# Layer 0's closing stage: the last pair's out_proj and transposes earlier, in_proj in two places, 24 unread products on TensorE

## The chip, the cores and the metric

One core of a Trainium2 chip runs the whole program. The time is device microseconds (us) of one execution, given as the median of several. The profile is of one further execution. TensorE (PE) does matrix products and transposes and writes PSUM. VectorE (DVE), ScalarE (ACT) and GpSimd (POOL) do elementwise work and reductions; SyncE (SP) issues most of the transfers. Each engine takes its own instructions in order.

## The reference, cut to what matters

Two layers run over an image of 64 x 64 tokens of 96 channels. Each layer is a mixer with a residual, and then a small quantized MLP with a residual:

```
x = x + L0_conv(ln_c(x))          # layer 0: in_proj 96 -> 192 + 192, depthwise 3x3 conv, SiLU,
                                  # four selective scans, layernorm, * silu(z), out_proj 192 -> 96
t = x + L0_ffn(ln_t(x))           # 96 -> 384, relu, 384 -> 96; operands rounded to 8 bits
x = t + L1_conv(ln_c(t))          # layer 1: in_proj, full 3x3 conv 192 -> 192, SiLU, four scans,
x = x + L1_ffn(ln_t(x))           #          * silu(z), out_proj; then the MLP again
```

The change lies at the end of layer 0: the layernorm of its mixer, the gate, out_proj, its MLP, and then the layernorm and the in_proj of layer 1.

## The kernel before

The 4096 tokens are 8 chunks of 512. `self.res` keeps the residual of all of them in SBUF, tokens on partitions. `back0` closes layer 0. It works on pairs of chunks: pair 0 is chunks 0 and 2, pair 1 is 1 and 3, pair 2 is 4 and 6, pair 3 is 5 and 7. A loop over `s` from -1 to 4 staggers the pairs: in step `s`, the mixer's statistics of pair `s + 1` stand beside out_proj and MLP of pair `s`, and beside layer 1's transposes and in_proj of pair `s - 1`.

What a step calls, with the lines of before:

- `centred(s + 1)`: products with a matrix of 1/192 (tiles `m`, L1075 and L1077) give the mean, DVE subtracts it, ACT squares (`sq`), POOL multiplies by the gate.
- `gated_sums(s)`: the product with the out_proj weights (tiles `oc`, L1110 and L1112), copied to SBUF by ACT (`ot`).
- `gated_out(c)`: four transposes (`o`, L1124), four DVE instructions that scale and add to the residual (L1127), and then `norm_chunk` for the MLP (tiles `lnmb`, `lnxcb`, `lnsqb`, `lnvb`, `lnrb`, `lnxnb`) with a cast on POOL (`xb`, L1981).
- `to_layer1(c)`: four transposes of a chunk that has its MLP behind it (`tr`, L188), a copy by ACT (`xt`, L189) and a store that SP issues (L1135).
- `keep_in_proj(c)`: layer 1's in_proj (`in`, L331), two products of 96 x 512 for a chunk; ACT copies one and DVE the other into the padded image `pad` (L333).
- `variance(s + 1)`: three products that sum the squares (`ov`, L1093), a root on ACT (`osd`), two small transfers, a reciprocal on DVE (`or`).
- `mlp_turn`, `mlp_up`, `mlp_down`: four transposes (`tf`), three products of 96 x 512 bf16 (`h`, L2000) with casts and relu on ACT, DVE and POOL, and twelve small fp8 products (`of`, L2020). After `mlp_down` the residual is added on DVE, and `norm_chunk` makes layer 1's input (tiles `lnmc` to `lnxnc`).

TensorE's order is the order of the source (`keep` enters each product into it). DVE, ACT, POOL and SP are ordered by the compiler's scheduler, so moving a call moves instructions on these engines too. PSUM tiles rotate in small pools: three buffers for `m` and `in` (tag `a`), two for `oc` and `h` (tag `h`), two for `ov`, `o` and `of` (tag `o`), one for `tr` and `tf` (tag `t`). A tile waits until the last reader of the one before it in its buffer is done.

After the loop, layer 1 begins with the product `spread4p` (L1197) and its convolution (`cw`, L1230), which reads the padded image of all chunks.

Of the kernel before, what the change touches and what calls it, by code (L numbers as in the profile page):

```python
# [28 lines left out]
F32 = mybir.dt.float32  # L29
# [10 lines left out]
P = 128  # L40
# [8 lines left out]
CH = 512  # L49
# [71 lines left out]
class Net:  # L121
# [897 lines left out]
    def back0(self):  # L1019

        tc = self.tc
        self.xn_d = self.scratch("xn1", [CD, L])
        with ExitStack() as ctx:
            self.tp = ctx.enter_context(tc.tile_pool(name="af0", bufs=3))
            self.lp = ctx.enter_context(tc.tile_pool(name="al0", bufs=2))  # L1030
            self.pa = ctx.enter_context(tc.tile_pool(name="ps_a0", bufs=3, space=PSUM))
            self.po = ctx.enter_context(tc.tile_pool(name="ps_o0", bufs=2, space=PSUM))
            self.ph = ctx.enter_context(tc.tile_pool(name="ps_h0", bufs=2, space=PSUM))
            self.pt = ctx.enter_context(tc.tile_pool(name="ps_t0", bufs=1, space=PSUM))
            self.w_in = self.w_in1
            n = NCH // 2
            self.sq, self.factor, self.xb, self.xn, self.xt, self.hid = {}, {}, {}, {}, {}, {}

            def chunks(s):
                c0 = s // 2 * 4 + s % 2  # L1040
                return (c0, c0 + 2) if 0 <= s < n else ()

            for s in range(-1, n + 1):
                if s + 1 < n:
                    self.centred(s + 1, chunks(s + 1))
                if 0 <= s < n:
                    self.gated_sums(s, chunks(s))
                for k in range(2):
                    for c in chunks(s - 1)[k : k + 1]:
                        self.to_layer1(c)  # L1050
                    for c in chunks(s)[k : k + 1]:
                        self.gated_out(c)
                for c in chunks(s - 1):
                    self.keep_in_proj(c)
                sums = self.variance(s + 1, chunks(s + 1)) if s + 1 < n else iter(())
                next(sums, None)
                for c in chunks(s):
                    self.mlp_turn(0, c)
                    self.mlp_up(0, c, lambda: next(sums, None))
                for _ in sums:  # L1060
                    pass
                for c in chunks(s):
                    self.mlp_down(0, c)
                    self.xn[c] = self.norm_chunk(self.lp, c, self.eps6, F32, f"c{c}")

    def keep(self, instruction):
        self.tc.keep_in_program_order(instruction)
# [1042 lines left out]
```

## Time and profile before

| | |
|---|---|
| median of 8 runs | 1451.32 us |
| lowest and highest | 1445.39 and 1462.72 us |
| the profiled execution | 1454.14 us, span 1452.3 us, mean TensorE clock 0.852 |
| `back0` in that execution | about 123.8 to 247.2 us from the start of the span |

The span runs from the first to the last instruction. In `back0` a step of the loop takes 24 to 27 us, and the last, which has only pair 3's layer 1 work left, 13.4 us (233.8 to 247.2). PEclk is the TensorE clock that was granted, 1.00 being full speed; in this stage the records show only 1.00 and 0.50, so a value between them is the share of time at either. A count of products in the trace is in passes: an f32 product appears as two MATMUL records. Idle time in square brackets is that of the engine just before an instruction, with what ended it.

### The profile page before, as it was taken

The numbers are of one execution on the slowest core, as the hardware profiler recorded it, in microseconds if no ns is written. First come the engines' busy times: TensorE is split into PE (matmuls) and PEld (weight loads), VectorE is DVE, ScalarE is ACT, GpSimd is POOL, SyncE is SP. The second block draws the span as 40 slices with busy tenths as digits, with TensorE's granted clock in tenths as the row PEclk, the third lists the DMA queues.
The fourth block names the chain that finished last, engine by engine and source line by source line (L and its number), as shares of the span: only waits on it lengthen the run. The fifth ranks groups of instructions, "written<-read, shape, count | busy, mean of one in ns | idle before, by whom it ended". The sixth has DMA issues, their size and how long they took to land. (4 is left out here: it accounts for less than half of the span.)

```text
span 1452.3 us, 12894 instructions
## 1 busy us (share of the span) xinstructions
PE 1156.0 (80%) x3976; PEld 467.2 (32%) x3976; DVE 1155.0 (80%) x887; ACT 909.9 (63%) x1099; POOL 785.4 (54%) x461
## 2 busy tenths in 40 slices
PE   7997777999991677787776777677778888899875
PEld 4532233333330222222222222222223333344343
DVE  6494674033169999999999999999999999999875
ACT  4455653044266677777777776777777777778444
POOL 1002321000005877687778776787878677885445
PEclk8999886999995889888888888878889998978855
DMA  2143000024059453735374457455555547442201
GB/s 64 47 143 72 11 17 17 15 54 124 22 164 286 140 185 127 221 111 181 127 246 124 137 175 226 136 161 178 170 182 157 169 135 239 147 129 89 71 2 42
DMA packets 68850, 183.19 MB, mean 126 GB/s; under 512 B 21488, under 2 KB 35460, under 8 KB 61956
## 3 DMA queue, kind: packets, MB, share of 16 engines
q1 hardware_dynamic: 67480, 182.00, 40.4%
q8 instruction: 33, 0.54, 0.2%
q10 hardware_dynamic: 1292, 0.28, 0.1%
q14 instruction: 45, 0.37, 0.1%
HBM read 155.98 MB, written 20.47 MB: 121 GB/s over the span
## 5 line engine op out<-in xcount | busy, mean ns | idle before, releaser
L1573 POOL TENSOR_TENSOR hss<-h1s,xws 128x1024 f32<-128x1024 f32 x96 | 224.5, 2375 | 135.5 <-PE hs L1581 135.5
L1557 ACT ACTIVATE da<-dt1s,a 128x1024 f32<-128x1024 f32 x168 | 187.9, 1119 | 139.9 <-DVE xws L1568 83.9
L1581 PE MATMUL hs<-hss,ident 128*128 128x512 f32 x376 | 216.3, 659 | 53.5 <-POOL hss L1573 33.1
L1568 DVE TENSOR_TENSOR_SCAN xws<-da,xws 128x1024 f32<-128x1024 f32 x96 | 224.2, 2335 | 10.4 <-DVE xws L1568 2.7
L1557 ACT ACTIVATE da<-dt0s,a 128x1024 f32<-128x1024 f32 x168 | 187.4, 1115 | 70.6 <-DVE xws L1568 52.3
L1581 PE MATMUL hs<-h0s,ident 128*128 128x512 f32 x376 | 203.5, 624 | 0.1
L1568 DVE TENSOR_TENSOR_SCAN h1s<-da,h1s,xws 128x1024 f32<-128x1024 f32 x72 | 169.2, 2350 | 11.0 <-ACT da L1557 2.3
L1581 PEld LDWEIGHTS hs<-hss,ident 128*128 128x128 f32 x376 | 70.5, 204 | 186.3 <-issue 81.8
L1396 POOL TENSOR_TENSOR dun<-u,dtn 128x512 f32<-128x512 f32 x4 | 5.9, 1482 | 197.2 <-DVE dtn L1293 107.6
L1581 PEld LDWEIGHTS hs<-h0s,ident 128*128 128x128 f32 x376 | 76.0, 203 | 100.3 <-issue 95.8
L1602 PE MATMUL acc<-hc2s,fold 128*32 128x512 f32 x128 | 47.5, 831 | 61.3 <-POOL hc2s L1591 58.2
L1602 PE MATMUL acc<-hc0s,fold 128*32 128x512 f32 x128 | 46.8, 820 | 52.9 <-POOL hc0s L1591 52.9
L1602 PE MATMUL acc<-hc1s,fold 128*32 128x512 f32 x128 | 45.5, 798 | 51.3 <-POOL hc1s L1591 51.3
L1541 POOL TENSOR_TENSOR x1s<-x1s,dus 128x1024 f32<-128x1024 f32 x32 | 75.0, 2360 | 9.1 <-DMA x1s<-bc 9.1
L1541 POOL TENSOR_TENSOR x2s<-x2s,dus 128x1024 f32<-128x1024 f32 x32 | 75.2, 2364 | 6.2 <-DMA x2s<-bc 6.2
L1568 DVE TENSOR_TENSOR_SCAN x0s<-da,x0s 128x1024 f32<-128x1024 f32 x32 | 74.7, 2335 | 4.3 <-ACT da L1557 1.9
L1568 DVE TENSOR_TENSOR_SCAN x1s<-da,x1s 128x1024 f32<-128x1024 f32 x32 | 74.7, 2335 | 3.6 <-ACT da L1557 1.0
L1568 DVE TENSOR_TENSOR_SCAN x2s<-da,x2s 128x1024 f32<-128x1024 f32 x32 | 74.7, 2335 | 3.3 <-ACT da L1557 0.7
L1581 PE MATMUL hs<-x0s,ident 128*128 128x512 f32 x128 | 67.4, 609 | 0.3 <-DVE x0s L1568 0.3
L1581 PE MATMUL hs<-x1s,ident 128*128 128x512 f32 x128 | 66.4, 601 | 0.0
L1541 POOL TENSOR_TENSOR x0s<-x0s,dus 128x1024 f32<-128x1024 f32 x28 | 65.8, 2363 | 0.0
L1253 PE MATMUL cv<-pad,cw 128*128 128x512 f32 x144 | 64.3, 598 | 0.0
(346 smaller groups left out, 2355.0 us busy)
## 6 DMA issues: line engine op xcount, KB each, us to landing
c0s<-bc SPq DMA_DIRECT2D x184, 128.0 KB, 2.5
c1s<-bc SPq DMA_DIRECT2D x184, 128.0 KB, 2.6
x2s<-bc SPq DMA_DIRECT2D x32, 512.0 KB, 4.9
x0s<-bc SPq DMA_DIRECT2D x28, 512.0 KB, 3.9
x1s<-bc SPq DMA_DIRECT2D x28, 512.0 KB, 6.6
dus<-du SPq DMA_DIRECT2D x20, 512.0 KB, 7.0
dt1s<-dt SPq DMA_DIRECT2D x40, 256.0 KB, 6.4
dt0s<-dt SPq DMA_DIRECT2D x40, 256.0 KB, 4.8
```

What stands on the lines that cost most here:

```text
L1253: keep(nc.tensor.matmul(t, cw[0][:, tap, 0:P], v, start=tap == 0, stop=False))
L1396: keep(nc.gpsimd.tensor_tensor(dun, u[1][:, m], dtn, ALU.mult))
L1541: keep(nc.gpsimd.tensor_tensor(x, x, du[:, part[j]], ALU.mult))
L1557: keep(nc.scalar.activation(das[i, s], dts[o][:, part[j]], AF.Exp, scale=self.a6[:, g, k : k + 1]))
L1568: keep(nc.vector.tensor_tensor_scan(to, da, x, start, ALU.mult, ALU.add))
L1573: keep(nc.gpsimd.tensor_tensor(cols(hs)[:, w, :], grid(h1)[:, w, :], grid(xw)[:, w, :], ALU.add))
L1581: keep(nc.tensor.matmul(t, self.ident, x[:, chunk(m)], start=x is hs, stop=x is xs[i % 3]))
L1602: keep(nc.tensor.matmul(to, self.fold4, src, start=k == 0, stop=k == NK - 1))
```

## The change

Steps -1, 0, 2, 3 and 4 are edited; step 1 is as before.

- In step 2, `gated_sums` of pair 3 is called between the two `mlp_down` calls, and no longer at the start of step 3.
- In step 3, `gated_out` of both chunks of pair 3 stands ahead of `to_layer1` of pair 2 (before, they alternated, `to_layer1` first). The in_proj of chunk 4 follows its transposes at once; the in_proj of chunk 6 stands after the MLP's first part of chunk 5.
- In step 4, the in_proj of a chunk follows its own transposes at once (before, both chunks were transposed first).
- `awake(n)` issues `n` products of 128 x 128 f32 into a PSUM tile of tag `a` that nothing reads: 4 in step -1 after `centred`, 6 in step 0 after the first product of `variance`, 4 in step 3 after `gated_out`, and 10 in step 4 ahead of the transposes.

```diff
             for s in range(-1, n + 1):
+                last = s == n - 1
                 if s + 1 < n:
                     self.centred(s + 1, chunks(s + 1))
-                if 0 <= s < n:
+                if 0 <= s < n and not last:
                     self.gated_sums(s, chunks(s))
-                for k in range(2):
-                    for c in chunks(s - 1)[k : k + 1]:
+                if s == -1:
+                    self.awake(4)
+                if last:
+                    for c in chunks(s):
+                        self.gated_out(c)
+                    self.awake(4)
+                    for c in chunks(s - 1):
                         self.to_layer1(c)
-                    for c in chunks(s)[k : k + 1]:
-                        self.gated_out(c)
-                for c in chunks(s - 1):
-                    self.keep_in_proj(c)
+                        if c == chunks(s - 1)[0]:
+                            self.keep_in_proj(c)
+                elif s == n:
+                    self.awake(10)
+                    for c in chunks(s - 1):
+                        self.to_layer1(c)
+                        self.keep_in_proj(c)
+                else:
...
                 sums = self.variance(s + 1, chunks(s + 1)) if s + 1 < n else iter(())
                 next(sums, None)
+                if s == 0:
+                    self.awake(6)
                 for c in chunks(s):
                     self.mlp_turn(0, c)
                     self.mlp_up(0, c, lambda: next(sums, None))
+                    if last and c == chunks(s)[0]:
+                        self.keep_in_proj(chunks(s - 1)[1])
...
                 for c in chunks(s):
+                    if s == n - 2 and c == chunks(s)[1]:
+                        self.gated_sums(n - 1, chunks(n - 1))
                     self.mlp_down(0, c)
...
+    def awake(self, products):
+
+        t = self.pa.tile([P, CH], F32, tag="a", name="awake")
+        for _ in range(products):
+            self.keep(self.nc.tensor.matmul(t[:, 0:P], self.mean, self.ident, start=True, stop=True))
```

No instruction on DVE, ACT, POOL or SP is added or removed. On DVE, pair 3's four-fold adds (L1127) and its MLP norms now lie between the residual adds and layer 1 norms of pair 2, and the copy of chunk 4's in_proj stands ahead of `lnxnb` of chunk 5. On ACT, both `ot` copies come ahead of chunk 6's `o16`. On POOL, `xb` of chunk 7 now follows two of chunk 5's `h8` casts. On SP, the store of chunk 5's `xt` goes ahead of the last of eight small loads (`a6`) of layer 1.

More of the change, by code (lines that the diff above doesn't have):

```diff
@@ L1043, in back0 @@
             for s in range(-1, n + 1):
+                last = s == n - 1
                 if s + 1 < n:
                     self.centred(s + 1, chunks(s + 1))
-                if 0 <= s < n:
+                if 0 <= s < n and not last:
                     self.gated_sums(s, chunks(s))
-                for k in range(2):
-                    for c in chunks(s - 1)[k : k + 1]:
-                        self.to_layer1(c)
-                    for c in chunks(s)[k : k + 1]:
-                        self.gated_out(c)
-                for c in chunks(s - 1):
-                    self.keep_in_proj(c)
+                if s == -1:
[5 more added lines that the diff above has]
+                    for c in chunks(s - 1):
+                        self.to_layer1(c)
+                        if c == chunks(s - 1)[0]:
[6 more added lines that the diff above has]
+                else:
+                    for k in range(2):
+                        for c in chunks(s - 1)[k : k + 1]:
+                            self.to_layer1(c)
+                        for c in chunks(s)[k : k + 1]:
+                            self.gated_out(c)
+                    for c in chunks(s - 1):
+                        self.keep_in_proj(c)
                 sums = self.variance(s + 1, chunks(s + 1)) if s + 1 < n else iter(())
                 next(sums, None)
+                if s == 0:
+                    self.awake(6)
                 for c in chunks(s):
```

## The prediction

> **What bounds the kernel now.** I read three views: busy time by stretch, to see what `back0` is bound by; TensorE's order of time in its end; and the granted clock in slices of 3.41 us.
>
> ```profile
> core 0: us, PE busy (x) PEld busy (x) DVE busy (x) ACT busy (x) POOL busy (x), PEclk, DMA share, GB/s
> 133.00:158.10 25.10, 17.83 (x69) 5.65 (x69) 11.81 (x30) 11.89 (x23) 9.44 (x12) 0.73 0.04 6
> 158.10:182.00 23.90, 18.34 (x89) 7.37 (x86) 18.66 (x44) 14.82 (x30) 8.85 (x11) 1.00 0.07 17
> ...
> 207.50:233.80 26.30, 18.79 (x73) 8.72 (x70) 16.47 (x40) 12.60 (x27) 4.95 (x8) 0.69 0.07 16
> 233.80:247.20 13.40, 7.55 (x20) 3.60 (x20) 6.20 (x13) 4.41 (x9) 0.00 (x0) 0.62 0.10 29
> 247.20:420.00 172.80, 171.48 (x641) 62.52 (x640) 41.25 (x64) 56.89 (x81) 3.81 (x3) 1.00 0.24 65
> ```
>
> No engine fills `back0`: it is a chain that changes engines, partly at a halved TensorE clock. From 247.2 TensorE is busy 171.48 of 172.80 us, so a microsecond gained or lost in `back0` reaches the end nearly whole; the scans behind it have no link to `back0` but its start.
>
> ```profile
> 213.42 0.61 PE L188 MATMUL tr<-ident,lnxnc 128*96 128x128 f32 x4 [1.76 <-DVE lnxnc L180]
> ...
> 216.90 6.96 PE L331 MATMUL in<-xt,w_in 96*128 96x512 f32 x8
> 223.69 0.39 PE L188 MATMUL tf<-identb,xb 128*96 128x128 bf16 x4
> ...
> 226.90 0.59 PE L188 MATMUL tf<-identb,xb 128*96 128x128 bf16 x4 [0.62 <-POOL xb L1981]
> ...
> 232.74 0.98 PE L2020 MATMUL of<-w2q,h 128*128 128x96 fp8e5 x10 [0.74 <-POOL h L2008]
> 238.10 1.06 PE L188 MATMUL tr<-ident,lnxnc 128*96 128x128 f32 x4 [4.38 <-DVE lnxnc L180]
> 239.83 1.09 PE L188 MATMUL tr<-ident,lnxnc 128*96 128x128 f32 x4 [0.67 <-ACT xt L189]
> 240.71 5.28 PE L331 MATMUL in<-xt,w_in 96*128 96x512 f32 x8
> 246.87 0.38 PE L1197 MATMUL spread4p<-ident,fold 128*32 128x128 f32 x2 [0.88 <-DVE pad L333]
> ```
>
> The same eight in_proj passes take 3.62 us at full clock (167.33, step 1), but 6.96 and 5.28 here. The 4.38 us in brackets is the wait for the norm.
>
> ```profile
> 138.27:141.68 3.41, 1.90 (x12) 1.00 0.00 0
> 141.68:145.09 3.41, 1.87 (x2) 0.50 0.01 2
> ...
> 148.51:151.92 3.41, 2.93 (x8) 0.50 0.00 0
> 151.92:155.33 3.41, 3.17 (x6) 0.50 0.00 0
> 155.33:158.75 3.42, 1.84 (x27) 1.00 0.04 1
> ...
> 182.64:186.05 3.41, 3.41 (x7) 0.50 0.00 0
> 186.05:189.47 3.42, 3.42 (x12) 1.00 0.00 0
> ```
>
> The columns are stretch, length, PE busy, clock. All changes of clock lie on one grid of 3.413 us. It halves after a slice about half busy or less (1.90, of which 1.21 is transposes), and returns after one nearly full (3.17 and 3.41; 2.93 did not do it).
>
> **The change part by part.** The sum is made against the profiled execution, 1454.14 us, which is 2.82 above the median of the runs.
>
> Price of an unread product: the 20 products of the same shape at the start (tile `warm`) take 6.34 us, their last twelve passes 1.28: 0.213 us a product at full clock. Half clock doubles that to 0.43.
>
> *Step -1, 4 products.* `m` ends at 128.51 and `ov` starts at 130.05, waiting for the squares: 1.54 us of cover for 0.85 (clock 1.00 from 128.03). 0 us; if the clock is still at half, 1.70 - 1.54 = +0.2.
>
> *Step 0, 6 products.* `ov` ends at 143.59 and `tf` waits for `xb` until 146.33: 2.74 us, for 2.55 at half clock. The slice 141.68 to 145.09 then holds 1.87 + 1.50 = 3.37 us of products, so full clock returns at 145.09 instead of 155.33. The MLP from there to its last product takes 11.94 us (146.33 to 158.27), and at full clock in step 1 9.52 (172.62 to 182.14): -2.4. But step 1's start moves on the grid, and that step had full clock throughout: a slice such as 155.33's, with 1.84 busy, is close to dropping. `m` at half clock cost 3.09 + 1.63 against 1.95 + 1.13 at 182: 1.6. I take half of that back: -1.5, between -2.4 and +0.4 (nothing warms, products late).
>
> *A rule that speaks against it.* The Trainium skill, "TensorE: Matmul & The Clock Gate", section "What's actually happening", has it that the clock rises after about 3.4 us of sustained work and drops after an idle window of that length. By this, no set but the last (4.3 us at half clock) can raise the clock alone, and filling a 0.9 us gap would keep nothing. The trace agrees on the rise (182.64 row) but not on the drop: 141.68 dropped after a slice with no gap over 0.95 us. By the rule step 0 is worth 0; by the rows up to -2.4. The measured rows decide, and the rule stays as the upper end.
>
> *Steps 2 and 3.* Both orders share the end of `mlp_down(4)`, 204.42. After it, the moved `oc` takes 1.96 + 1.10 = 3.06 at full clock, to 207.5 (before, at half clock for a part, 3.15 + 1.10, to 211.66); `mlp_down(6)` ends at 208.1 instead of 207.68. ACT now does both `ot` copies (0.58 each) ahead of `o16` of chunk 6: 209.7 instead of 208.2, so pair 2's second residual is 1.5 late. `o` of chunk 7 needs the buffer that `o16` frees: 209.8. The 4 products then end at 211.2 (213 at half clock); `tr` behind them waits for `lnxnc` of chunk 4 at about 211.2 anyway: 0 to +0.9, and off the path, because of what DVE has to do. From `lnxcc` of chunk 4 (ends 208.15) to `lnxnb` of chunk 5 the new order on DVE has 25 instructions: 7 reductions and centrings and 3 normalizations at 0.55, 8 adds of 0.30, 4 reciprocals of 0.2, `o16` 0.56, the residual 0.72, the `pad` copy 0.69; 10.7 us less 0.08 overlap each, 8.7, and three waits for ACT (squares, roots) of 0.4 to 0.5: `lnxnb` ends near 218.1, `xb` at 218.75, `tf` of chunk 5 starts at 218.8 instead of 223.69. That is -4.9 for the first chunk.
>
> It isn't kept. The in_proj of chunk 6 now stands on TensorE between the MLP of chunk 5 and `tf` of chunk 7, and is no longer covered by the norm. TensorE is nearly idle from 214 to 218.8 in the new order (one `tr`), so the clock is at half there: 218.8 + 0.7 `tf`, 0.7 ACT copy, three `h` with their waits 1.8, two in_proj products at 6.96/4 = 1.74 each: `tf` of chunk 7 at about 225.5 instead of 226.90. `xb` of chunk 7, behind two `h8` casts of 0.6 on POOL, is ready by 224.5 and doesn't decide. From there 6.82 us to the last `of`, as before. Sum -1.4; I take -1.0, between -2.8 (full clock) and +0.7 (the DVE copy of chunk 4's in_proj, on which `lnxnb` of chunk 5 and POOL's `xb` now queue, comes late).
>
> *Step 4.* The 10 products take 4.3 at half clock under the 4.38 us wait: 0 on the path, up to +0.2. Then the order: before, 238.10 to 247.17 = 9.07 us with the clock rising at 244.08. After: `tr` 1.06, ACT copy 0.65, two in_proj 3.5, `tr` 1.06, copy 0.65, 3.5, the last copy 0.9 (0.2 + 0.69): 11.3 at half clock, +2.2, because the second copy is no longer under an in_proj and no slice gets full. At full clock 0.64 + 0.65 + 1.8 + 0.64 + 0.65 + 1.8 + 0.9 = 7.1: -2.0. The products with the `of` ahead and the `tr` behind make some 5.2 us of work, and hold a whole slice of 3.41 at about half of the grid's positions. About even: 0, from -2.0 to +2.2, and +1.7 more if the convolution starts at half clock.
>
> *Queues.* Tag `a` has one more tile to rotate; the tiles it waits for were read microseconds before: 0. SP's last `a6` load waits for `xt` of chunk 5, some 14 us later than its seven fellows; only layer 1's scans, after 420, read it: 0.
>
> Sum: 0 - 1.5 - 1.0 + 0 = -2.5: 1451.6 for an execution like the profiled one. Less the 2.8 by which that lies above its median: **1449 us**. A measurement of this kernel can tell about 0.5% (7.3 us) from no change, so this counts as none.
>
> **The rivals.**
>
> *The clock stays up (faster).* If the sets together keep full clock from step 0 to the convolution: -2.4 (step 0), -1.6 (`m` at 182), -1.2 (`oc`, 3.15 to 1.96), -2.8 for steps 2 and 3, -2.0 (step 4): -10, about 1441. For it: each place where the clock fell is a slice about half busy, and all but one now get products. Against it: none is added in step 1 or in the start of step 2, nor between 214 and 219. Even half of the rest beyond my sum makes -6.
>
> *The split in_proj never warms (slower).* One mechanism: eight passes in a row filled a slice by themselves before (up at 223.5 and 244.08); two groups of 3.5 us with a 1.7 us gap don't, if the products miss a slice of the grid. Place: chunk 6's in_proj at 222 and step 4. Price: steps 2 and 3 +0.7, step 4 +2.2, convolution +1.7, and the same grid shift costing step 0's gain and one more `m` at half clock (+0.4, +1.6): +6.6, and more where the half clock spans two slices of the convolution (+1.7): 1459. It decides when the 4.3 us of products hold no full slice; against it, that is only half of the positions, and all terms have to come together.
>
> *It doesn't do what it says.* The waits that the products fill are ended by DVE and ACT; if the clock isn't on that path, they are worth 0 and only the order counts: -1.0 to +1.2, 1450 to 1452.
>
> **How the numbers follow.** Near zero (my sum, and the order alone) 0.51; clock kept, or enough of it, 0.33; slower by the split 0.16. The likeliest case by itself spans 1444 to 1457, from the ends above and the grid's position. The range for 8 in 10, 1439 to 1459, reaches to 1441 with 2 us of scatter below and to the slower rival.
>
> **What would show it.** Right: clock 1.00 in the slices behind `ov` in step 0, and its MLP near 9.5 us; `tf` of chunk 5 nearly 5 us sooner after `mlp_down(4)`, `tf` of chunk 7 only 1 to 2; half clock in chunk 6's in_proj; step 4 with 1.00 or 0.50 by the grid. Wrong: a loss or gain outside 120 to 250 us; `tr` held by the unread products; step 4 at full clock in every run.

## The result, and the profile after

The changed kernel takes 1445.08 us (median of 21 runs, 1439.28 to 1455.9) against 1452.1 us (58 runs of the kernel before): a ratio of 0.9943, 95% interval 0.9924 to 0.9962. On another chip it came to 0.9963, 0.9941 to 0.9986. It is faster, by about half a percent; the forecast was 1449 us and no clear change, with 0.33 for faster.

The profiled execution has a span of 1442.7 us, 9.6 less than the one before. `back0` runs from the first `m` to the first `cw` product: 121.89 to 240.72, 118.83 us, before 123.35. The same view of busy time by stretch, one row for step -1 and 0 together and one for each later step:

```profile
core 0: us, PE busy (x) PEld busy (x) DVE busy (x) ACT busy (x) POOL busy (x), PEclk, DMA share, GB/s
121.89:155.70 33.81, 26.67 (x103) 9.73 (x104) 14.54 (x34) 16.21 (x27) 13.14 (x18) 0.85 0.26 59
155.70:179.60 23.90, 18.33 (x85) 7.37 (x85) 18.65 (x44) 14.85 (x30) 8.87 (x11) 1.00 0.07 17
...
205.47:228.80 23.33, 15.39 (x72) 8.59 (x72) 15.95 (x39) 12.04 (x26) 5.04 (x8) 0.69 0.08 18
228.80:240.72 11.92, 8.89 (x38) 5.74 (x38) 6.21 (x13) 4.46 (x9) 0.00 (x0) 0.89 0.12 34
```

The row of before that answers to the first of these is

```profile
123.82:158.10 34.28, 25.35 (x82) 7.35 (x83) 14.38 (x34) 16.18 (x27) 13.15 (x18) 0.75 0.26 58
```

The clock rises in step 4 (0.89, before 0.62) and in the first stretch (0.85, before 0.75), not in step 3 (0.69 in both). TensorE's order of time in the end of `back0`, from the shared point, the end of `mlp_down(4)` at 201.88:

```profile
201.20 0.68 PE L2049 MATMUL of<-w2q,h 128*128 128x96 fp8e5 x12
201.71 2.12 PE L1139 MATMUL oc<-y,wg 128*96 128x512 f32 x4
...
209.91 1.98 PE L331 MATMUL in<-xt,w_in 96*128 96x512 f32 x4 [0.67 <-ACT xt L189]
212.88 0.61 PE L188 MATMUL tr<-ident,lnxnc 128*96 128x128 f32 x4 [0.98 <-DVE lnxnc L180]
215.50 0.66 PE L188 MATMUL tf<-identb,xb 128*96 128x128 bf16 x4 [2.01 <-POOL xb L2010]
...
218.53 3.62 PE L331 MATMUL in<-xt,w_in 96*128 96x512 f32 x4
221.94 0.63 PE L188 MATMUL tf<-identb,xb 128*96 128x128 bf16 x4
...
228.59 3.78 PE L1093 MATMUL awake<-ident,mean 128*128 128x128 f32 x20
233.18 0.61 PE L188 MATMUL tr<-ident,lnxnc 128*96 128x128 f32 x4 [0.81 <-DVE lnxnc L180]
234.46 1.98 PE L331 MATMUL in<-xt,w_in 96*128 96x512 f32 x4 [0.67 <-ACT xt L189]
```

Four in_proj passes take 1.98 us at full clock and 3.62 at half: chunk 6's, at 218.53, are at half, those of step 4 at full. The twenty passes of the ten unread products start at half and are over 0.81 us ahead of the norm, so nothing waits for them. `tf` of chunk 5 comes 13.6 us after the shared point (before 19.3), `tf` of chunk 7 20.1 (22.5). The clock in slices of its grid (stretch, length, PE busy, clock):

```profile
139.27:142.69 3.42, 2.56 (x14) 1.00 0.01 2
142.69:146.10 3.41, 1.03 (x7) 0.99 0.00 0
146.10:149.51 3.41, 2.74 (x7) 0.50 0.00 0
...
210.95:214.37 3.42, 1.56 (x7) 0.99 0.12 37
214.37:217.78 3.41, 1.61 (x6) 0.50 0.26 62
...
228.02:231.43 3.41, 3.41 (x24) 0.51 0.02 5
231.43:234.85 3.42, 1.94 (x14) 1.00 0.00 0
```

The products of step 0 keep the slice from 139.27 busy (2.56 us), but the next has only 1.03, and the clock falls behind it, at about 146. In step 4 the products, with the last `of` ahead of them, fill 228.02 to 231.43 whole, and the clock is up from there.

### The profile page after: what moved, and what is told of

Same layout as the page of the kernel before. It is cut to its first block, busy times and chain, and to the rows that moved or that the text cites. A ratio compares the mean times of both kernels' runs of the same rounds, so it can differ in the third digit from the quotient of the medians.

```text
span 1442.7 us, 12990 instructions
## 1 busy us (share of the span) xinstructions
PE 1152.7 (80%) x4024; PEld 468.8 (32%) x4024; DVE 1154.5 (80%) x887; ACT 909.8 (63%) x1099; POOL 785.8 (54%) x461
```

## The experiments

Two measures stand beside the ratio: the stage (first `m` to first `cw`), and step 4 (end of the last `of` to first `cw`). Both are from one profile of each run, and one profile depends on where the stage meets the grid. The scans of layer 1 are taken from the start of the first to the start of the last scan into the tile `h0s` (before: 459.2 to 1361.6).

**order_only**: all unread products out, the new order kept.

```diff
-                if s == -1:
-                    self.awake(4)
...
-                    self.awake(4)
...
-                    self.awake(10)
...
-                if s == 0:
-                    self.awake(6)
```

> The new order of work without any of the 24 unread products. Measure: the stage from the first m to the first cw product, 123.35 us before and 118.83 after in the two profiled executions. Theory A (the gain is the clock in step 4, bought by the ten products): the stage stays within 2 us of before, step 4 runs its in_proj at half clock (about 3.6 us a chunk), ratio to before 0.999 to 1.002. Theory B (the gain is the order): stage about 119 us, ratio 0.994 to 0.997.

Measured: 0.9994, interval 0.9967 to 1.002; stage 123.31 us, step 4 14.59. Its order of time in step 4:

```profile
236.49 1.06 PE L188 MATMUL tr<-ident,lnxnc 128*96 128x128 f32 x4 [4.38 <-DVE lnxnc L180]
238.22 3.78 PE L331 MATMUL in<-xt,w_in 96*128 96x512 f32 x4 [0.67 <-ACT xt L189]
241.80 1.06 PE L188 MATMUL tr<-ident,lnxnc 128*96 128x128 f32 x4
243.53 1.98 PE L331 MATMUL in<-xt,w_in 96*128 96x512 f32 x4 [0.67 <-ACT xt L189]
```

Without products the clock comes back only for the second chunk (theory A had both at half), and the serial order of step 4 is 1.1 to 1.5 us longer than before (13.09 to 13.45). The order alone buys nothing that this measurement can see. Its scans took 900.0 us, 2.4 less than before (more on this below), so an estimate from the medians (1451.39 against 1452.38) leaves the rest of the kernel over a microsecond longer.

**products_only**: the old order, with 4, 6, 4 and 10 products. The function `awake` is that of the change.

```diff
+                if s in (-1, 3, 4):
+                    self.awake({-1: 4, 3: 4, 4: 10}[s])
                 for k in range(2):
                     for c in chunks(s - 1)[k : k + 1]:
                         self.to_layer1(c)
...
+                if s == 0:
+                    self.awake(6)
```

> The old order of work with the 4, 6, 4 and 10 unread products in the waits (step -1, step 0, start of step 3, start of step 4). Theory A: most of the change's gain is here: step 4's in_proj at full clock (eight passes in about 3.7 us, before 5.28), stage 119 to 121 us, ratio 0.995 to 0.998. Theory B: no more than 1 us, ratio 0.999 to 1.000.

Measured: 0.9964, 0.9941 to 0.9987; stage 114.72 us, below the expected range, step 4 11.21.

```profile
230.34 3.90 PE L1074 MATMUL awake<-ident,mean 128*128 128x128 f32 x20
234.92 0.61 PE L188 MATMUL tr<-ident,lnxnc 128*96 128x128 f32 x4 [0.69 <-DVE lnxnc L180]
236.52 0.61 PE L188 MATMUL tr<-ident,lnxnc 128*96 128x128 f32 x4 [0.98 <-DVE lnxnc L180]
236.97 3.60 PE L331 MATMUL in<-xt,w_in 96*128 96x512 f32 x8
```

With full clock the old step 4 is the shorter one: both transposes are under the norm's wait, and only one copy lies open. The stage also had luck: the clock held from 158.3 to 223.1. By the medians most of the gain sits in the products (-5.0 us here, -1.0 in order_only); the intervals of the two overlap, so the ratios alone don't show it.

**only_ten**: the change without the 4, 6 and 4.

```diff
-                if s == -1:
-                    self.awake(4)
...
-                    self.awake(4)
...
-                if s == 0:
-                    self.awake(6)
```

> The change with only the ten products of step 4; the 4, 6 and 4 left out. Theory A: as the whole change, within 1.5 us (stage 118.5 to 121 us, ratio 0.994 to 0.997), because the six products of step 0 only put the fall of the clock off by a slice or so. If instead the six count: step 0's MLP at half clock throughout (11.9 us from its first tf to its last of), stage 2 us longer than with them, ratio 0.996 to 0.998.

Measured: 0.9976, 0.9955 to 0.9998; stage 119.53 us, step 4 11.93, step 0's MLP (first `tf` to last `of`) 11.58; in the four profiles of the change it is 11.30, 9.75, 9.47 and 10.68. The ratio favours some worth in the smaller sets, but the intervals of this and the change overlap; what the 4, 6 and 4 are worth stays open.

**v2**: chunk 6's in_proj right behind its transposes, three products between the second and third `h` of pair 3, and both transposes first in step 4.

```diff
                         self.to_layer1(c)
-                        if c == chunks(s - 1)[0]:
-                            self.keep_in_proj(c)
+                        self.keep_in_proj(c)
                 elif s == n:
                     self.awake(10)
                     for c in chunks(s - 1):
                         self.to_layer1(c)
+                    for c in chunks(s - 1):
                         self.keep_in_proj(c)
...
-                    self.mlp_up(0, c, lambda: next(sums, None))
-                    if last and c == chunks(s)[0]:
-                        self.keep_in_proj(chunks(s - 1)[1])
+                    self.mlp_up(0, c, (lambda: self.awake(3)) if last else lambda: next(sums, None))
```

> The change with three edits: chunk 6's in_proj at once after its transposes (into the idle time before tf of chunk 5), three unread products between the second and third h of each chunk of pair 3 (where earlier steps have an ov product), and in step 4 both transposes ahead of the four in_proj products. From the trace of the change: in_proj of chunk 6 at full clock in a wait of 2.0 us instead of 3.62 us at half clock on the path: -2 to -3; step 4 without the second copy in the open: -0.7. Stage 114.5 to 117 us, ratio to before 0.991 to 0.994. The rival: chunk 6's in_proj holds tf of chunk 5 by 0.7 us and the clock falls all the same: stage 118 to 119.5, ratio 0.994 to 0.996.

Measured: 0.9955, 0.9931 to 0.9979, which is the rival's ratio and can't be told from the change's; stage 115.62 us, as expected. Step 3 did what was expected: chunk 6's in_proj at full clock (1.98), and 26.9 us from chunk 6's `tf` to the last `of`, in the change 30.0 to 30.5. Step 4 gave 2 us of it back, at 13.89:

```profile
231.89 2.46 PE L1091 MATMUL awake<-ident,mean 128*128 128x128 f32 x20
236.44 0.99 PE L188 MATMUL tr<-ident,lnxnc 128*96 128x128 f32 x4 [2.08 <-DVE lnxnc L180]
238.09 1.09 PE L188 MATMUL tr<-ident,lnxnc 128*96 128x128 f32 x4 [0.67 <-ACT xt L189]
238.98 5.78 PE L331 MATMUL in<-xt,w_in 96*128 96x512 f32 x8
```

The clock was up when the ten products came, so they were over in 2.46 us; TensorE then idled 2.08 us, the slice from 233.12 had 1.33 us busy, and the clock fell at 236.5. Ten products are sized for a wait that begins at half clock.

**v3**: v2 with products that wait for the norm's own tiles, so that they spread over the wait.

```diff
-                    self.awake(10)
+                    self.awake(5, 5, 5)
+                    self.awake(0, 7, 4)
...
-                    self.awake(6)
+                    self.awake(6, 2, 4)
...
-    def awake(self, products):
+    def awake(self, products, after=None, more=0):
...
+        for _ in range(more):
+            self.keep(self.nc.tensor.matmul(t[:, 0:CD], self.mean, self.centre[after], start=True, stop=True))
```

`awake(5, 5, 5)` issues 5 products at once and 5 of 96 columns on chunk 5's centred tile (`lnxcc`, kept as `self.centre[5]`).

> The kernel v2 with its unread products spread over the waits by their operands: in step 0, six as before and then four of 96 columns that read the centred tile of chunk 2; in step 4, five at once, five that read the centred tile of chunk 5 and four that read that of chunk 7. In v2's profile the ten products of step 4 ran at full clock, were over in 2.1 us of a wait of 4.4, and the clock fell at the next grid point. If the clock is what counts in step 4, v3 keeps it there: step 4 10.8 to 11.5 us instead of 13.9, stage from first m to first cw 112 to 115 us, ratio to before 0.990 to 0.994. The rival: products that wait for DVE hold the transposes behind them by 1 to 2 us, and the stage stays at 115 to 118 us, ratio as v2 (0.9955).

Measured: 0.9933, 0.9908 to 0.9957; stage 114.12 us, step 4 11.21, step 0's MLP 9.59.

```profile
236.81 1.35 PE L1093 MATMUL awake<-ident,mean 128*128 128x128 f32 x10
238.60 1.35 PE L1095 MATMUL awake<-lnxcc,mean 128*128 128x96 f32 x10 [0.45 <-DVE lnxcc L173]
240.68 1.10 PE L1095 MATMUL awake<-lnxcc,mean 128*128 128x96 f32 x8 [0.72 <-DVE lnrc L179]
241.62 0.60 PE L189 MATMUL tr<-ident,lnxnc 128*96 128x128 f32 x4
242.95 0.61 PE L189 MATMUL tr<-ident,lnxnc 128*96 128x128 f32 x4 [0.73 <-ACT xt L190]
243.40 3.60 PE L332 MATMUL in<-xt,w_in 96*128 96x512 f32 x8
```

No gap in these lines is longer than 0.73 us, and the clock holds to the convolution. The ratio is in the expected range, but its interval overlaps the change's. This execution began its stage late, at 134.07, which brought the next run.

**v4**: v3 with two products ahead of each in_proj in the opening loop.

```diff
+                fill = pm.tile([P, CH], F32, tag="m", name=f"fill{old}")
+                for _ in range(2):
+                    keep(nc.tensor.matmul(fill[:, 0:P], self.ident, self.ident, start=True, stop=True))
                 t[old] = [pm.tile([P, CH], F32, tag="m", name=f"in0{old}{g}") for g in range(2)]
```

> The kernel v3 with two unread products ahead of in_proj in each turn of layer 0's opening loop, outside the change. In six profiles the start of the closing stage lies between 121.9 and 133.2 us, with the opening at half clock for 7 us in the one and 34 us in the other. If that clock sets the start, it comes at 119 to 123 us here, the spread between runs shrinks, and the ratio is another 0.002 to 0.004 below v3. The rival: DVE and ACT set the opening's time, the products only lengthen it: start 124 to 127 us, ratio as v3 or 0.001 above.

Measured: 0.9908, 0.9875 to 0.9941, in 7 runs between 1437.55 and 1442.84; start of the stage 121.76, stage 114.11. The opening still had 6.8 us at half clock. It was measured again beside the change:

> v4 once more beside the changed kernel, on one chip, since its first interval (7 runs) overlaps that of the change. If the clock of the opening is what spreads the runs: median 1438 to 1442 us, range under 10 us, ratio to before 0.989 to 0.992, and a start of the stage between 120 and 124 us in the profile. Rival: the first seven runs were lucky: range 15 us or more, ratio as the change.

Measured: 1439.65 us, 0.9898, 0.9855 to 0.9941, 6 runs between 1433.69 and 1441.93; start 118.88 (earlier than expected, with no half clock in the opening), stage 116.18. On the same chip the change:

> The changed kernel once more, beside v4: ratio to before 0.993 to 0.996, runs spread over 15 us or more, in the profile a stage of 116 to 120 us with step 4 at 11.9 to 12.2 us, and the scans at 899 to 900.5 us. If step 4 comes to 14 us, the ten products do depend on where they meet the grid.

Measured: 1446.5 us, 22 runs between 1438.49 and 1456.03, 0.9963; start 121.70, stage 116.63, step 4 11.94. v4 has the lowest ratio here, but its interval overlaps v3's and only touches the change's (at 0.9941). Its 6 runs lie within 8.2 us where the 22 of the change spread over 17.5; fewer runs spread less, but none of v4's 13 runs on both chips is above 1442.84, and 14 of those 22 are, as are 7 of v3's 19.

**after_again and before_again**: both kernels once more, for the grid.

> The changed kernel once more, for a second profile at another position of the clock's grid. If the ten products raise the clock only where they hold a whole slice of 3.41 us, step 4 is either 11 to 12 us (full clock) or 14 to 15.6 us (half clock), and the stage 117 to 123 us by that and by step 0.

Measured: stage 116.72 us (just under the expected 117), step 4 11.94.

> The kernel before once more, for a second profile. Its stage moves with the grid too: 120 to 126 us, and the start of the stage between 120 and 134 us; the scans behind the convolution differ by up to 3 us without any change in them.

Measured: stage 122.46 us, step 4 13.41, start of the stage 127.98. The scans took 902.3 us, not a scattered value: 902.4, 902.3 and 902.0 in the three profiles so far with the old order (before, this one, products_only), 899.2 to 900.4 in all with the new. That asked for a cause.

**before_plus1 and after_plus127**: unread memsets of one column on DVE, during the convolution.

```diff
                 u1 = self.conv_narrow(kp, ps, up, c)
+                if c == 0:
+                    idle = up[1].tile([P, 1], F32, tag="idle", name="idle")
+                    for _ in range(1):
+                        self.keep(self.nc.vector.memset(idle, 0.0))
```

In after_plus127 the range is 127.

> The kernel before with one unread one-column memset more on DVE, in the convolution, where DVE idles for over 20 us. In the profiles so far the scans (first to last scan into h0) take 902.0 to 902.4 us in the kernels with the old order and 899.3 to 900.4 in those with the new; the old have six waits of 0.46 us on DVE, 155 us apart, each time at the same scan of a group, in which no other engine is named as the releaser. Theory C: this comes from where the group's instructions lie in DVE's stream (by the waits listed, the new order has about one instruction more ahead of the scans): one instruction more takes the six waits away, scans 899.3 to 900.5 us. Rival: it comes from SP's order of transfers (the store and the small load that changed places): nothing changes here, scans 902 to 902.5, six waits of 0.46. The median is no help: 2.4 us in 1452.

Measured: scans 900.1 us; ratio 0.9975, 0.9951 to 1.0; stage 116.66 and start of the stage 120.64, in the old order and without unread products. The waits of DVE in the scans (who waited for whom, us in total, times, longest), of the kernel before and of this one:

```profile
DVE xws L1568 <- DVE xws L1568: 2.3, 5, 0.5
DVE h1s L1568 <- ACT da L1557: 2.3, 6, 0.6
...
```

```profile
DVE x0s L1572 <- ACT da L1561: 2.0, 5, 0.6
DVE h1s L1572 <- ACT da L1561: 1.9, 5, 0.6
DVE x1s L1572 <- ACT da L1561: 1.3, 4, 0.6
DVE x2s L1572 <- ACT da L1561: 0.9, 2, 0.5
```

The row in which `xws` waits for itself is gone (a sixth wait lies outside the window of that view). The order of the work on ACT, POOL and SP is that of the kernel before, so SP's order is not the cause: one memset in DVE's stream is enough (it also brings a tile of one column in SBUF, which the new order does not).

> The changed kernel with 127 such memsets in the same place. A group of scans takes some 128 instructions of DVE with its waits, so if the six stalls come back with a period of one group (theory C), 127 more put the stream where the kernel before had it: six waits of 0.46 us, scans 902 to 902.5 us. If only the neighbourhood of the change or SP's order counts: scans as in the change, 899.3 to 900.4.

Measured: scans 899.8 us, no such waits; ratio 0.997, 0.9945 to 0.9995; stage 117.06. The stalls did not come back, but the count was one off. In the three traces that have the six waits, counted with DVE's semaphore instructions, 593, 721, 849, 977, 1105 and 1233 instructions stand ahead of them: exactly 128 apart. Ahead of the first scan stand 507 in these three, 508 in before_plus1, 509 in the change, whose source adds nothing on DVE but whose stream has two semaphore instructions more, and 636 here. That is 129 more than 507: by a period of 128 it is the place of before_plus1, which has no waits, and 126 memsets would have been that of before. So the runs fit a period of 128 instructions, but the run that would test it isn't there, and what the 0.46 us are stays open.

**All profiles together.** The stage follows the time that it spends at half clock, in the old order and in the new:

| old order | half clock, us | stage, us | new order | half clock, us | stage, us |
|---|---|---|---|---|---|
| before | 47.8 | 123.35 | order_only | 44.4 | 123.31 |
| before_again | 40.8 | 122.46 | only_ten | 39.8 | 119.53 |
| before_plus1 | 27.3 | 116.66 | after | 30.7 | 118.83 |
| products_only | 20.5 | 114.72 | after_plus127 | 27.3 | 117.06 |
| | | | after_again, after_more | 23.9 | 116.72, 116.63 |
| | | | v2, v4_more | 17.1 | 115.62, 116.18 |
| | | | v3, v4 | 12.5 | 114.12, 114.11 |

A single profile of the old order without products, before_plus1, is as short as the change's. What the order does to the stage beside its half-clock time doesn't show here. The table alone doesn't prove the direction, since a longer stage also has room for more half clock; the runs that add products to a fixed order (products_only, only_ten, v3) do for step 4.

## Why the prediction was right and wrong, point by point

The time lies in the range and the sign was right, but the case named as likeliest was no clear change; the sum, -2.5 us, was too small. Two of the prediction's own signs of being wrong came true: step 4 at full clock in every profile, and a gain outside 120 to 250 us. From the profiles (three of the old order's `back0`: before, before_again, before_plus1; four of the change's: after, after_again, after_more, after_plus127):

- *Step -1, 0 us*: right. The products end before `ov`, which starts 6.2 us after the first `m` in both.
- *Step 0, -1.5*: right in size. The last `of` of step 0 comes 33.9 us after the first `m` before and 32.8 after (means), -1.1. The mechanism came as forecast in two of the four profiles, after_again and after_more: the products completed the slice at half clock, full clock came behind it, and the MLP took 9.75 and 9.47 us (9.52 forecast). In after_again:

```profile
140.53:143.95 3.42, 1.91 (x12) 1.00 0.00 0
143.95:147.36 3.41, 3.37 (x9) 0.50 0.01 2
147.36:150.78 3.42, 2.28 (x15) 1.00 0.00 0
```

  In the other two the clock had not fallen before the products, which put off the fall instead of ending it (MLP 11.30 and 10.68; before 11.94, 11.11 and 11.11).
- *The trace over the rule of the Trainium skill ("TensorE: Matmul & The Clock Gate", "What's actually happening"), on the drop*: held. The clock fell after slices that were part busy, 142.69 to 146.10 with 1.03 us being one (its longest idle time is 2.05), where the rule wants an idle window of about 3.4 us; and filling short waits kept it up (v3). In the stage of all 14 profiles the clock fell only after slices with 0.74 to 2.02 us busy, and held only after slices with 1.65 or more.
- *"Returns after one nearly full" slice*: not sharp. In before itself it stayed at half after a full one:

```profile
216.77:220.18 3.41, 3.41 (x7) 0.50 0.24 60
```

  And in step 4 of after_again it rose after one with 2.81 (229.28 to 232.69), less than the 2.93 that did not do it. Busy time in the trace isn't all that decides the rise.
- *Steps 2 and 3, -1.0*: the mechanism was right. `tf` of chunk 5 came 5.6 us sooner after `mlp_down(4)` (4.9 forecast), and chunk 6's in_proj was at half clock in all four profiles and ate most of it. From chunk 6's `tf` in step 2 to the last `of` it is 30.2 us on average, before 31.5: -1.3. Before took 32.8 twice and 28.8 once, when the clock happened to hold; the new order never held it. Three profiles against four don't settle this term.
- *Step 4, "about even: 0"*: the term that failed. All four took 11.92 to 12.14 us, before 13.09 to 13.45: -1.3. I gave the ten products a full slice at half of the grid's positions, counting 5.2 us of work. What the profiles show is full clock for in_proj in every one: step 3 always ends at half clock, so the products last 3.4 to 4.6 us under the wait, and the slice that holds most of them (3.41, 2.81, 3.27 and 3.41 us busy) is followed by full clock. That 2.81 is enough was not in the prediction's reading of the rise. v2, which arrives at full clock, shows the other side.
- *"The scans behind it have no link to `back0` but its start"*: wrong. They took 902.2 us with the old order (before, before_again, products_only) and 899.7 with the change (means), -2.6, which the six waits of 0.46 us make up. I had looked at what a moved instruction waits for, not at what its place in a stream does to a loop 300 us later.
- *The queues, 0*: right for tag `a`, POOL and SP.

The parts sum to -0.9 at the end of step 2 (what is left of step 0's -1.1), -1.3, -1.3 and -2.6: about -6.1, against -7.0 and -4.3 by the two pairs of medians. So `back0` itself gave about -3.5, near the forecast -2.5; much of what made the change clear of the noise is the term that the prediction put at nothing, and that it went the right way was luck. The rival "the clock stays up" was nearest: right in step 4 and in two of four profiles for step 0, wrong for step 3. The slower rival, the split in_proj, is there in step 3 and in order_only's step 4, and pays its price only without the ten products. The other 1.9 us between the two profiled executions lie before the change, in the opening.

## What to carry to other kernels

In a chain of short stages, price each TensorE stretch at both clocks, and ask of every grid slice of 3.4 us whether it is full enough to keep the clock; a filler of fixed length is right for one clock only, so tie it to the tiles of the wait that it fills. Moving work ahead of the path is lost when what it displaces lands on the path at half clock: put the displaced piece into a wait. Before believing a gain of a few us from one pair of profiles, take several and measure the stage, since this one moved by 6.7 us between two profiles of the same code (before and before_plus1, whose memset comes after it).

## What was not expected of the hardware

By these profiles the spread between runs comes largely from the clock in the opening of layer 0, over 70 us ahead of the change. Time at half clock there, and start of the stage: 3.4 us and 120.64 (before_plus1), 6.8 and 121.89 (after), 10.2 and 123.82 (before), 20.5 and 127.98 (before_again), 34.1 and 133.21 (only_ten), 37.5 and 134.07 (v3): about 0.4 us for each. v4's longer opening lies on the same line, with 0 and 118.88 (v4_more) and 6.8 and 121.76 (v4). From the start of the stage on, the four profiles of the change take 1318.5 to 1320.8 us, while their starts differ by 4.9. At half clock most slices of the opening's loop have 2.7 us busy in v3, and the clock stays; it stayed after two slices of 3.41 us too, so why it stays is not settled. And six waits of 0.46 us on DVE came and went with one instruction more in its stream.
